# Self-products of 4096 rows on one core: adjacent rows for a partition, the last tile outside the loop, and its last columns in sixteen small stores

## The chip, the cores and the metric

One NeuronCore of a Trainium2 chip. The metric is the device time of the whole program in microseconds, median of several executions. The other cores are idle.

## The reference

```python
# inputs: (4096, 256) float32
dot = jnp.einsum('bi,bj->bij', inputs, inputs)
iu, ju = jnp.triu_indices(256)
return dot[:, iu, ju]                 # (4096, 32896) float32
```

Every row gives its 256 x 257 / 2 = 32896 products. 4.19 MB come in, 538.97 MB go out.

## The kernel before

A batch tile is 128 rows, one row for a partition. A row's products are 256 runs: run i is `x[i:]` times the scalar `x[i]`. VectorE and ScalarE share the runs, and a third of the 32896 columns is collected in each of three output buffers, then stored by one DMA from the sync engine's queue. Tile 0 is written out ahead of the loop, tiles 1 to 31 are the loop.

```python
x_in = x.rearrange("(g p) d -> p g d", p=P)          # tile g = rows 128 g to 128 g + 127
x_out = [v.rearrange("(g p) c -> g p c", p=P) for v in dram_disjoint_views(out, PIECES)]
xt = xpool.tile([P, groups, d], F32, name="x")
cuts = [0, 1, groups // 2, groups]
for a, b in zip(cuts, cuts[1:]):
    nc.sync.dma_start(xt[:, a:b], x_in[:, a:b])      # three input loads
...
def batch_tile(x_of, g, first):
    for c, (lo, hi) in enumerate(zip(borders, borders[1:])):
        o = opool.tile([P, hi - lo], F32, tag=f"o{c}", name=f"o{c}")   # bufs=1
        cuts = [lo, *(first if c == 0 else []), hi]
        for a, b in zip(cuts, cuts[1:]):
            shares.even()
            for _, i, j, at, length in runs(d, a, b):
                shares.multiply(o[:, at - lo : at - lo + length], x_of, j, i, length)
            dest = x_out[c][bass.ds(g, 1), :, a:b].rearrange("o p c -> p (o c)")
            nc.sync.dma_start(dest, o[:, a - lo : b - lo])

batch_tile([xt[:, 0], xt[:, 0]], 0, FIRST)
with tc.For_i(1, groups, 1, ..., iteration_sync="reg_based") as g:
    ...                                              # copies of x for each engine
    batch_tile([xv, xa], g, [])
```

## Time and profile before

| | before |
|---|---|
| time, median | 1292.98 us (1292.86 when the prediction was made) |
| profiled span | 1290.7 us |
| read and written | 4.19 and 538.97 MB, 421 GB/s over the span |
| busy VectorE, ScalarE | 77%, 76% |
| loop period, from landing records | 39.8 us |

The time is read from the stores, not from the compute rows; the prediction shows the lines. The landing records of this kernel hold 1632 additions to semaphores for its 102 DMAs, 16 for each; a DMA's landing is here the moment of the last one. They are read as one from each of the 16 DMA engines: of the run's last store 15 come between 1279.10 and 1279.27 us, and one at 1289.10, when the DMA share has long been that of a single engine (0.05). Two more views of the page of the kernel before are used below. First the DMA issues (size in KB, then us from issue to landing), of which the input loads matter:

```profile
x<-in_r_inputs_dram SPq DMA_DIRECT2D x1, 2048.0 KB, 13.6
...
x<-in_r_inputs_dram SPq DMA_DIRECT2D x1, 1920.0 KB, 8.2
```

Both loads are issued within the first 2 us, so the larger number is about the moment at which all input has landed: 15.3 us. The stores land after it, from 16.97 us on. Second, who made VectorE wait (total us, times, longest us):

```profile
DVE o L52 <- DMA out_dram<-o: 259.7, 62, 4.8
```

62 waits in 31 trips, none over 4.8 us: VectorE waits for the landing that frees a buffer twice a trip. That is 260 of its 300 us of idle time; most of the rest is the end, when its work is done and the stores still run.

### The profile page before, as it was taken

What the parts mean: (1) busy time and instruction counts of PE and PEld (TensorE: products, weight loads), DVE (VectorE), ACT (ScalarE), POOL (GpSimd) and SP (SyncE); (2) the same over time, 40 slices, a digit from 0 to 9 for tenths busy, and PEclk for the clock granted to TensorE, in tenths of its full rate; (3) what the DMA queues carried; (4) which work ended last, traced back from release to release, by engine and by line L of the source; (5) the groups of instructions that cost most, each with busy time, mean ns of one, the idle gap of its engine ahead of it and who ended that gap; (6) DMA issues with size and microseconds to landing.
All of it is one profiled execution on the core that took longest, in us unless ns stands there. A gap on an engine that the chain in (4) does not pass through costs nothing.

```text
span 1290.7 us, 9881 instructions
## 1 busy us (share of the span) xinstructions
DVE 990.8 (77%) x4992; ACT 981.0 (76%) x3330; POOL 0.2 (0%) x4
## 2 busy tenths in 40 slices
DVE  9878787787877788777878778787787877788771
ACT  9778787787877788777878778787787877788771
POOL 0000000000000000000000000000000000000000
DMA  9999999999999999999999999999999999999996
GB/s 373 433 434 432 433 435 434 432 435 434 433 433 435 416 434 416 413 435 434 415 413 435 423 424 415 424 424 433 415 413 435 413 433 415 434 415 413 435 424 259
DMA packets 18405, 543.21 MB, mean 421 GB/s; under 512 B 1632, under 2 KB 5728, under 8 KB 5856
## 3 DMA queue, kind: packets, MB, share of 16 engines
q1 hardware_dynamic: 18400, 543.17, 98.0%
q14 instruction: 5, 0.04, 0.0%
HBM read 4.19 MB, written 538.97 MB: 421 GB/s over the span
## 4 chain that ended last, share of the span: by engine, by line
DMA 59%; DVE 38%; issue 0%; DVEq 0%; SPq 0%
DMA out_dram<-o 59%; DVE o L52 38%; DMA x<-in_r_inputs_dram 0%; DVEq L52 0%; SPq L108 0%; DVEq L112 0%; DVEq L149 0%; DVEq L122 0%
## 5 line engine op out<-in xcount | busy, mean ns | idle before, releaser
L52 DVE TENSOR_SCALAR o<-xv 128x256 f32<-128x256 f32 (+63 forms) x4805 | 951.2, 281 | 267.1 <-DMA out_dram<-o 259.7
L58 ACT ACTIVATE o<-xa 128x255 f32<-128x255 f32 (+63 forms) x3193 | 936.6, 386 | 278.6 <-DMA out_dram<-o 272.4
L52 DVE TENSOR_SCALAR o<-x 128x150 f32<-128x150 f32 (+50 forms) x156 | 30.6, 279 | 3.0 <-DMA x<-in_r_inputs_dram 3.0
L58 ACT ACTIVATE o<-x 128x255 f32<-128x255 f32 (+52 forms) x105 | 30.4, 385 | 0.9 <-DMA x<-in_r_inputs_dram 0.9
L124 ACT ACTIVATE xa<-x 128x256 f32 x31 | 12.9, 416 | 3.4
L122 DVE COPY xv<-x 128x256 f32 x31 | 9.1, 294 | 4.0
L58 ACT ACT_TABLE_LOAD x1 | 1.3, 1283 | 0.7 <-PEq L140 0.7
L140 POOL MEMSET const-bfloat16-1.0<- 128x1 bf16 x1 | 0.1, 101 | 0.0
L140 POOL MEMSET const-uint8-127<- 128x1 uint8 x1 | 0.1, 101 | 0.0
L140 POOL MEMSET const-float32-0.0<- 128x1 f32 x1 | 0.1, 98 | 0.2 <-issue 0.2
L140 POOL MEMSET const-float32-1.0<- 128x1 f32 x1 | 0.1, 98 | 0.0
## 6 DMA issues: line engine op xcount, KB each, us to landing
out_dram<-o SPq DMA_DIRECT2D x63, 5472.0 KB, 30.1
out_dram<-o SPq DMA_DIRECT2D x32, 5504.0 KB, 24.7
x<-in_r_inputs_dram SPq DMA_DIRECT2D x1, 2048.0 KB, 13.6
out_dram<-o SPq DMA_DIRECT2D x1, 2048.0 KB, 14.2
x<-in_r_inputs_dram SPq DMA_DIRECT2D x1, 1920.0 KB, 8.2
out_dram<-o SPq DMA_DIRECT2D x1, 1888.0 KB, 18.2
out_dram<-o SPq DMA_DIRECT2D x1, 1024.0 KB, 9.9
out_dram<-o SPq DMA_DIRECT2D x1, 512.0 KB, 13.1
```

What stands on the lines that cost most here:

```text
L52: self.nc.vector.tensor_scalar(dst, x[:, j : j + length], x[:, i : i + 1], None, ALU.mult)
L58: self.nc.scalar.activation(dst, x[:, j : j + length], AF.Copy, scale=x[:, i : i + 1])
L122: nc.vector.tensor_copy(xv, now)
L124: nc.scalar.activation(xa, now, AF.Copy)
L140: nc = _bacc.Bacc("TRN2", target_bir_lowering=False, num_devices=1)
```

## The change

Its intent, as far as the text tells: make each partition's input contiguous; write the last tile out so that its stores can be shaped; and shape the last ones, perhaps so that the DMA engines end together.

```diff
-    x_in = x.rearrange("(g p) d -> p g d", p=P)
+    x_in = x.rearrange("(p g) d -> p g d", p=P)
...
-        v.rearrange("(g p) c -> g p c", p=P) for v in dram_disjoint_views(out, PIECES)
+        v.rearrange("(p g) c -> g p c", p=P) for v in dram_disjoint_views(out, PIECES)
...
+                if b == width and last:
+                    b -= LAST                                   # LAST = 256
+                store(c, g, a, b, o[:, a - lo : b - lo])
+        if last:
+            p0 = 0
+            for k in [*range(1, 16), 8]:
+                store(c, g, b, hi, o[p0 : p0 + k, b - lo :], p0, p0 + k)
+                p0 += k
...
-        groups,
+        groups - 1,
...
+    final = xt[:, groups - 1]
+    batch_tile([final, final], groups - 1, [], last=True)
```

More of the change, by code (lines that the diff above doesn't have):

```diff
@@ L63 @@
 PIECES = 3
+LAST = 256
 FIRST = [1024, 3072, 7168]
@@ L97, with store, batch_tile @@
     shares = Shares(nc)
-    def batch_tile(x_of, g, first: list[int]):
+    def store(c, g, a, b, src, p0=0, p1=P):
+        dest = x_out[c][bass.ds(g, 1), p0:p1, a:b].rearrange("o p c -> p (o c)")
+        nc.sync.dma_start(dest, src)
+    def batch_tile(x_of, g, first: list[int], last: bool = False):
         for c, (lo, hi) in enumerate(zip(borders, borders[1:])):
@@ L106, in batch_tile @@
                     shares.multiply(o[:, at - lo : at - lo + length], x_of, j, i, length)
-                dest = x_out[c][bass.ds(g, 1), :, a:b].rearrange("o p c -> p (o c)")
-                nc.sync.dma_start(dest, o[:, a - lo : b - lo])
+                if b == width and last:
[6 more added lines that the diff above has]
+                p0 += k
     batch_tile([xt[:, 0], xt[:, 0]], 0, FIRST)
```

## The prediction

> **What bounds the kernel now.** I read the page first (busy rows, DMA rows, queues), then the sync engine's waits, then a table of stretches over the end, then the landing and packet records of single DMAs in the trace.
>
> ```profile
> DVE  9878787787877788777878778787787877788771
> ACT  9778787787877788777878778787787877788771
> DMA  9999999999999999999999999999999999999996
> GB/s 373 433 434 432 433 435 434 432 435 434 433 433 435 416 434 416 413 435 434 415 413 435 423 424 415 424 424 433 415 413 435 413 433 415 434 415 413 435 424 259
> ...
> q1 hardware_dynamic: 18400, 543.17, 98.0%
> ```
>
> The reader is to see that VectorE and ScalarE are idle a quarter of the time, that the 16 DMA engines are busy in every slice but the last, and that the ceiling is about 435 GB/s. 538.97 MB must be written, so the kernel is bound by its stores. Compute only has to stay ahead of them.
>
> ```profile
> SPq L108 <- DVE o L52: 1192.2, 96, 19.2
> SPq L112 <- DMA out_dram<-o: 23.6, 2, 12.9
> SPq L108 <- ACT o L58: 4.2, 2, 3.9
> ```
>
> The second line matters most. At the loop's exit the sync engine waits 23.6 us for the landings of the last trip's DMAs. In this kernel nothing follows the loop, so that wait is only the drain [...].
>
> ```profile
> 1264.90:1276.10 11.20, 0.00 (x0) 0.00 (x0) 0.00 (x0) 1.00 1.02 440
> 1276.10:1279.30 3.20, 0.00 (x0) 0.00 (x0) 0.00 (x0) 1.00 0.54 234
> 1279.30:1289.10 9.80, 0.00 (x0) 0.00 (x0) 0.00 (x0) 1.00 0.05 22
> 1289.10:1290.70 1.60, 0.00 (x0) 0.00 (x0) 0.00 (x0) 1.00 0.00 0
> ```
>
> (Columns: stretch, length, busy of VectorE, ScalarE, GpSimd, clock, DMA share, GB/s.) In the last 9.8 us of transfers the share is 0.05, one engine of 16. The landing records say the same of the whole run: each DMA adds 16 to its semaphore, and the last addition falls behind the median one by 0.4 us for the input, 2.4 us in the first trips, 6.3 us at 240 us, and about 10.5 us from the middle of the run on, where the single set of output buffers stops it growing. A fast engine needs 24 packets of 1.618 us = 38.8 us for a trip; the slow one needs 39.84 us, which is the period of the loop. That slow engine never idles between 3 us and 1289.1 us, so it sets the time. Its packets take about 1.67 us while VectorE and ScalarE run and 1.62 us while they idle.
>
> [...]
>
> **The change part by part.**
>
> *Row mapping.* A partition's 32 rows are adjacent, so the second and third input loads become one piece of 15 KB and one of 16 KB for a partition in place of 31 of 1 KB. In the records, the 248 pieces of an engine took from 2.93 to 14.8 us, 11.85 us for 4.06 MB. At the 434 GB/s that stores reach this is 9.36 us. The stores queue behind the loads without a gap (landings at 16, 18.6, 23.4, 27.9, 40.8, 53.8 us), and their data is ready in time (issues at 10.5, 18.8, 33.6 us, the last one limited by compute, all ahead of their turn even if the queue is 2.5 us earlier). So the slow engine's whole chain moves forward: **-2.5 us**. The SBUF side of the stores is the same. On the HBM side the pitch is 32 x 131584 B = 4112 KiB = 4 MiB + 16 KiB, and I take the rate as unchanged.
>
> *The last tile outside the loop.* The order of the changed program shows that the sync engine's branch out of the loop waits for all three store semaphores of the loop and for a barrier of all engines, and that VectorE's and ScalarE's last tile comes after this barrier. So the 23.6 us wait, harmless before, now stands in the middle: no compute of tile 31 and no store of it until the slow engine has landed tile 30. The stall of the slow engine, from its last packet of tile 30 to its first of tile 31:
> - last packet's end to landing, 0.46 us (1288.64 to 1289.10 at the end of before);
> - barrier, 0.55 us (last landing 1289.12, release 1289.67);
> [...]
> - compute of the first third before anything can be stored, 7.4 us (1225.55 to 1232.93 in the last trip);
> - issue to first packet, 1.0 us (0.74 to 1.76 us at the start).
>
> Sum **+9.9 us**. After that the queue stays full: the second store is issued 8.5 us and the third 23.5 us after the first, while two stores take 25.9 us. The tile itself takes the slow engine what it took before (39.4 us from landing to landing), less 1 KB for each of 8 partitions if that engine gets no small store: **-0.3 us**.
>
> *The 16 small stores.* Seven of them (1 to 7 partitions) go out right behind the main store and hide under it. [...] the order shows the store of 8 partitions waiting for lane 3, which is that of the last 10752-column store. It can be issued only when the slow engine has landed that. The stores of 8 to 15 partitions then follow one another at 0.44 to 0.47 us (the spacing of issues at 9.53, 10.00 and 10.47 us), and the final one of 8 partitions shares lane 3 with the first of 8. Its issue comes 8 x 0.44 = 3.5 us after the main landing; issue to landing about 1.9 us (1.0 to the first packet, 0.4 for its latency as in the first load's packets, 0.5 to the landing). **+5.4 us**, with almost no bytes: 128 KB.
>
> Sum: 1292.86 - 2.5 + 9.9 - 0.3 + 5.4 = 1305.4, so I say **1305 us**, a ratio of 1.009.
>
> **The rivals.**
> 1. *HBM addresses decide.* [...] If that took 5% of the store rate, the time would be about 1305 + 62 = 1367 us. [...] About 7%.
> 2. *The slow engine is cured.* If its slowness came from the addresses of the rows that it writes, the new mapping would give 38.8 us a trip: about 31 x 1.0 us less, 1305 - 31 = 1274 us, still within 2%. Against: its packets are slow exactly while compute runs, and in the last 9.8 us, when nothing else runs, its packets follow at 1.624 us; that is no property of addresses. About 5%.
> 3. *The drain is hidden.* If the lag of the slow engine, or the last tile's compute, could run across the barrier, the stall would vanish and the kernel would gain: 1292.9 - 2.5 - 0.3 + 5.4 = 1295.5 us, or 1290 us if the small stores hid too. Against: the waits in the order. About 5%.
> 4. *The small stores even out the end*, which is perhaps their intent: [...] after the drain the lag starts from zero and is only about 1 us in one tile.
>
> **Range and chances.** The uncertain terms within my account are [...] the tail of small stores (3 to 8 us, since the issue cost of a DMA with 8 to 15 partitions isn't in the trace), and the gain of the loads (1 to 3 us). Together some 4 us to either side; rivals 2 and 3 pull the low end further. Range 1297 to 1311 us. Slower by over 2% means above 1318.7 us, which only rival 1 gives: 0.07. Faster by over 2% means below 1267.0 us, which would need rival 2 and hidden stalls at once: 0.03. Within 2%: 0.90.
>
> **What the profile will show.** The input loads landing at about 12.5 us in place of 15.3. A loop period of 39.8 us as before. VectorE and ScalarE idle for over 10 us before the last tile, with the DMA share falling to one engine and then to 0 for about 8 us near 1250 us; the sync engine's wait at the loop's exit shorter than the span's end. A last tile whose slow engine trails by 1 us, not 10. Then some 5 us at the end with nearly no bytes, stores 8 to 15 spaced by under half a microsecond. A changed period of the loop would prove me wrong about addresses; a busy DMA row straight through 1250 us would prove me wrong about the drain; a last store that lands right after the main one would prove me wrong about the lanes.

What is cut out told of the hardware what no trace or run had shown: which engines a DMA runs on, what a large pitch does, rules for semaphores and drains. One term of the sum is among it, my guess of 0.5 us for the jump to the code behind the loop. The four terms of the stall that are left make 9.4 us (0.46 + 0.55 + 7.4 + 1.0); with the cut one the stall came to +9.9 and the whole to 1305.4 us, as it stands. A lane is the semaphore to which a DMA reports: in the trace of the kernel before, the nine DMAs ahead of the loop report to eight semaphores in turn, the ninth to that of the first; the lanes are counted from 0.

## The result, and the profile after

1304.89 us (1304.81 to 1305.06, 4 runs) against 1292.98 us: a ratio of 1.0092, 95% interval 1.0075 to 1.011. All ratios here are the mean time of one kernel's fast runs over that of the other's of the same rounds, so not quite the ratio of the medians quoted. By the 2% rule this is "same"; by the interval it is clearly a little slower. The result was correct.

The sync engine's waits of the changed kernel (total us, times, longest us):

```profile
SPq L125 <- DMA out_dram<-o: 23.5, 2, 12.9
SPq L103 <- DMA out_dram<-o: 10.7, 1, 10.7
```

The first line is the 23.6 us drain of before, unchanged, but work now follows it. The second is new: one store waited 10.7 us for another to land. It is the store of 8 partitions: in the trace it waits for the semaphore of the main store, to which it reports too; the main store landed at 1297.55 us, and this one was issued at 1297.56. Next, what ended VectorE's waits in the changed kernel:

```profile
DVE o L52 <- DMA out_dram<-o: 250.3, 59, 4.8
DVE o L52 <- PEq L165: 25.2, 1, 25.2
DVE o L52 <- DVE xv L135: 6.8, 29, 0.2
```

The second line is a wait that the kernel before did not have: once, for 25.2 us. It names TensorE, which does no work in this kernel. That is the barrier at the loop's exit, put down to whoever updated its semaphore last; what held the barrier was the sync engine, and what held the sync engine was the landing of tile 30 (1248.33 us; the first product of tile 31 starts at 1249.16). Here is where an inferred releaser has to be followed one step further.

Stretches of the end of the changed kernel (length, busy of VectorE, ScalarE, GpSimd, clock, DMA share, GB/s):

```profile
1238.60:1247.90 9.30, 0.00 (x0) 0.00 (x0) 0.00 (x0) 1.00 0.05 24
1247.90:1257.50 9.60, 8.25 (x34) 8.34 (x23) 0.00 (x0) 1.00 0.00 1
1257.50:1296.10 38.60, 22.25 (x122) 21.65 (x82) 0.00 (x0) 1.00 1.01 433
1296.10:1297.20 1.10, 0.00 (x0) 0.00 (x0) 0.00 (x0) 1.00 0.10 24
1297.20:1301.90 4.70, 0.00 (x0) 0.00 (x0) 0.00 (x0) 1.00 0.09 22
1301.90:1303.10 1.20, 0.00 (x0) 0.00 (x0) 0.00 (x0) 1.00 0.00 0
```

This is the whole story in six lines. The slow engine drains tile 30 alone (share 0.05); nothing moves for 9.6 us while the first third of tile 31 is computed; the last tile is stored at 433 GB/s; the slow engine ends about 1 us after the others, not 10; then 4.7 us at 22 GB/s for the small stores.

### The profile page after: what moved, and what is told of

It reads as the page before. It is cut to its first block, busy times and chain, and to the rows that moved or that the text cites. A ratio compares the mean times of both kernels' runs of the same rounds, so it can differ in the third digit from the quotient of the medians.

```text
span 1303.1 us, 9865 instructions
## 1 busy us (share of the span) xinstructions
DVE 990.3 (76%) x4991; ACT 980.4 (75%) x3329; POOL 0.2 (0%) x4
## 5 line engine op out<-in xcount | busy, mean ns | idle before, releaser
L52 DVE TENSOR_SCALAR o<-xv 128x256 f32<-128x256 f32 (+63 forms) x4650 | 920.5, 282 | 257.5 <-DMA out_dram<-o 250.3
L58 ACT ACTIVATE o<-xa 128x255 f32<-128x255 f32 (+63 forms) x3090 | 906.4, 386 | 268.7 <-DMA out_dram<-o 262.7
L52 DVE TENSOR_SCALAR o<-x 128x249 f32<-128x249 f32 (+34 forms) x311 | 61.1, 281 | 28.1 <-PEq L165 25.2
L58 ACT ACTIVATE o<-x 128x18 f32<-128x18 f32 (+50 forms) x208 | 60.4, 383 | 26.0 <-PEq L165 25.1
L137 ACT ACTIVATE xa<-x 128x256 f32 x30 | 12.5, 416 | 3.3
```

Of the source, the lines that this page charges most:

```text
L52: self.nc.vector.tensor_scalar(dst, x[:, j : j + length], x[:, i : i + 1], None, ALU.mult)
L58: self.nc.scalar.activation(dst, x[:, j : j + length], AF.Copy, scale=x[:, i : i + 1])
L137: nc.scalar.activation(xa, now, AF.Copy)
```

## The experiments

Twelve kernels were run. "Mapping alone" is the kernel before with only the two `rearrange` lines changed.

### Taking the change apart

**Mapping alone.**

```diff
-x.rearrange("(g p) d -> p g d", p=P)
+x.rearrange("(p g) d -> p g d", p=P)        # and the same for the output
```

> The mapping alone, in the kernel before (loop over all 31 further tiles, no last tile outside, no small stores). Theory (the mapping only shortens the input loads, and the store period stays 39.8 us): in the changed kernel the loop's landing of tile 30 came 1.40 us earlier than before (1248.33 against 1249.73), so 1292.98 - 1.4 = 1291.6 us, ratio 0.9989. Rival A (the 4112 KiB pitch also changes the store rate, hidden in the sum): a loop period off 39.8 us by more than 0.1 us and a time off by more than 3 us. Rival B (the mapping is neutral): 1293.0 us.

Measured: 1291.82 us against 1292.98, ratio 0.999 (0.9977 to 1.0004). The interval includes 1, but every one of the five runs (1291.6 to 1291.93) lies below every one of before (1292.92 to 1293.29). The loads' lines are now

```profile
x<-in_r_inputs_dram SPq DMA_DIRECT2D x1, 2048.0 KB, 12.6
...
x<-in_r_inputs_dram SPq DMA_DIRECT2D x1, 1920.0 KB, 7.0
```

1.0 and 1.2 us shorter. Two stretches of the loop of 39.84 us each, 400 us apart, are both filled by the work of one trip:

```profile
500.00:539.84 39.84, 30.94 (x157) 30.59 (x105) 0.00 (x0) 1.00 0.98 423
900.00:939.84 39.84, 30.97 (x157) 30.61 (x105) 0.00 (x0) 1.00 0.98 423
```

The first of them in the kernel before:

```profile
500.00:539.84 39.84, 30.95 (x158) 30.60 (x106) 0.00 (x0) 1.00 0.99 424
```

The landing records measure the period itself: it is (1288.16 - 54.16) / 31 = 39.81 us; the kernel before has (1289.10 - 55.42) / 31 = 39.80. So the HBM addresses of the stores changed nothing, and the gain is the loads'.

**The last tile outside the loop alone** (old mapping, whole stores).

```diff
-        groups,
+        groups - 1,
...
+    final = xt[:, groups - 1]
+    batch_tile([final, final], groups - 1, [])
```

> The last tile outside the loop alone: old mapping, whole stores. Theory (drain and barrier put the last tile's first third of compute between two stores): from the landing of tile 30 to that of tile 31 the changed kernel took 49.22 us, the kernel before 39.37, so +9.85 us, less nothing for small stores: 1292.98 + 9.9 = 1302.9 us, ratio 1.0077. Rival (the cost of the change sits in the small stores, the last tile is hidden by the stores still queued): 1293 to 1294 us.

Measured: 1301.91 us, ratio 1.007 (1.0056 to 1.0084): +8.9 us, a microsecond less than expected. The landings of tiles 30 and 31 are 49.51 us apart (1249.55 and 1299.06), close to the 49.22 foreseen, but the span ends 1.1 us after the last landing, not 1.6 as before: the loop-exit barrier that used to stand after the last landing is now in the stall. I had counted it as new. That is about half of the microsecond; the rest is not explained.

**Mapping and last tile, without the small stores.**

```diff
-    batch_tile([final, final], groups - 1, [], last=True)
+    batch_tile([final, final], groups - 1, [])
```

> The changed kernel without its small stores (the last store whole, 11008 columns). Theory: 1292.98 - 1.4 + 9.9 = 1301.5 us, which is 3.4 us below the changed kernel. Rival (the small stores are free because they are 128 KB in 543 MB): 1304.9 us.

Measured: 1300.7 us, ratio 1.0059. The parts add up: 1291.82 + 8.93 = 1300.75. The small stores therefore cost 1304.89 - 1300.7 = 4.2 us.

**Four small stores in place of sixteen.**

```diff
-            for k in [*range(1, 16), 8]:
+            for k in [32] * 4:
```

> The changed kernel with the last 256 columns in four stores of 32 partitions in place of 16 stores of 1 to 15 and 8. Same bytes, but lanes 4 to 7 are free, so no small store waits for the main one. Theory (the tail is the wait for lane 3 and the issues after it): all four land right behind the main store, 1301.5 us plus at most 0.5, that is 1301.5 to 1302.0. Rival (each small store costs by itself, 4.3 us for 16): a quarter of the tail stays, 1302.4 to 1302.8 us. Rival (rows of 1 KB are what costs): 1304.9 us.

Measured: 1300.96 us, 0.3 us above the kernel with no small stores. The same 128 KB in the same rows of 1 KB cost almost nothing once no store has to wait for a lane. Its end:

```profile
1296.40:1297.70 1.30, 0.00 (x0) 0.00 (x0) 0.00 (x0) 1.00 0.19 57
1297.70:1299.00 1.30, 0.00 (x0) 0.00 (x0) 0.00 (x0) 1.00 0.00 0
```

The last bytes have moved by 1297.4 us, the last store has landed at 1298.14, and the program ends at 1299.0; the 4.7 us of trickle are gone. So bytes and row length cost 0.3 us at most, and "a quarter of the tail for a quarter of the stores" is wrong too. The run changes the number of stores and their shape together with the lanes. That the lane is the cause is read from the changed kernel itself: after its wait of 10.7 us nine stores are issued one behind the other, in 3.3 us, and in this run no store waits so.

### What the stall is made of

**Two tiles outside the loop** (small stores as in the change).

```diff
-        groups - 1,
+        groups - 2,
...
+    final = xt[:, groups - 2]
+    batch_tile([final, final], groups - 2, [])
     final = xt[:, groups - 1]
```

> The changed kernel with two tiles outside the loop in place of one (small stores as in the change). Theory (the cost is one drain and barrier at the loop's exit, whatever follows it): no second stall, 1304.9 us give or take 0.5. Rival (code outside the loop is slow by itself[...]): a second stall of up to 8.9 us, 1310 to 1314 us.

Measured: 1304.33 us, half a microsecond *below* the changed kernel. One drain, one stall:

```profile
1198.60:1208.50 9.90, 0.00 (x0) 0.00 (x0) 0.00 (x0) 1.00 0.05 22
1208.50:1217.90 9.40, 8.43 (x35) 8.53 (x23) 0.00 (x0) 1.00 0.18 75
1217.90:1297.30 79.40, 52.56 (x276) 51.47 (x184) 0.00 (x0) 1.00 0.96 414
```

The picture is that of the changed kernel, one tile earlier, and the two tiles after it run through at 414 GB/s. Code outside the loop is not slow here; leaving the loop is what costs, 9.4 us in this run.

**The first third of the last tile in four stores.**

```diff
-    batch_tile([final, final], groups - 1, [], last=True)
+    batch_tile([final, final], groups - 1, FIRST, last=True)     # [1024, 3072, 7168]
```

> The changed kernel with the first third of the last tile cut into stores of 1024, 2048, 4096 and 3776 columns as in the first tile, so that the first store of the last tile waits for 0.9 us of compute and not for 7.5. Theory (compute of the first third is the largest part of the stall): the stores now start 6.5 us earlier, but the last third's data is ready only 29 us after the barrier, as before (the main store was issued at 1278.06 and its engines were still busy until 1283.9); the main store then begins 1 us after its issue and lands at about 1292.8 in place of 1297.55: 1304.9 - 4.8 = 1300.1 us. Rival (the stall is the barrier and the jump, not compute): 1304 to 1305 us.

Measured: 1299.27 us, 5.6 us below the changed kernel where 4.8 was expected; the main store landed at 1292.39 us (expected 1292.8). The stall:

```profile
1247.90:1250.90 3.00, 1.57 (x6) 1.66 (x5) 0.00 (x0) 1.00 0.01 3
```

By 1250.9 us five or six products of each engine are made, and the first packet follows at 1251.1, not 1257.5. So most of the stall was the 7.5 us of compute behind the barrier, and the old lesson of tile 0 (cut the first store small) holds after this drain too, for 5.6 us. It doesn't give back the whole stall because the last third's data is then what is late: all 16 engines end the main store within 0.14 us of one another, none of them lagging.

### Where the slow DMA engine comes from

**Almost no compute in the loop** (mapping alone). Its output is wrong, which doesn't matter for the time.

```diff
-                for _, i, j, at, length in runs(d, a, b):
+                for _, i, j, at, length in list(runs(d, a, b))[:most]:   # 2 in the loop
```

(The three output buffers are allocated once, so that what is stored has been written.)

> The mapping alone with only the first two of each third's products computed in the loop; a wrong result on purpose, same stores, same waits, almost no VectorE and ScalarE work. Theory (the slow engine's packets are stretched from 1.62 to 1.67 us by running compute): the lag hardly grows, the period is 38.8 to 38.9 us, time 1260 to 1263 us. Rival (that engine is slow by itself or by its rows' addresses): 1291.8 us, lag of 10 us at the end.

Measured: 1263.82 us, ratio 0.9774. A trip:

```profile
500.00:538.90 38.90, 1.17 (x4) 1.81 (x4) 0.00 (x0) 1.00 1.00 433
```

The stores are the same bytes to the same addresses, now at 433 GB/s in place of 423, and the last engine trails the median one by 0.6 us at the end, not by 10. The period from landings is (1260.36 - 54.43) / 31 = 38.90 us. Running compute is what makes one engine slow here: 39.81 us a trip with it, 38.90 without. The run also lets the store queue get deeper, but the earlier packets of the kernel before (1.67 us beside compute, 1.62 us without, on a queue that never emptied) say that depth isn't it.

**One engine's compute only** (same). Their outputs are wrong, which doesn't matter for the times.

```diff
+            if only == "scalar":      # in the vector branch; "vector" in the scalar branch
+                return                # all but the first two products of a third
```

> The mapping alone with ScalarE's products left out of the loop but the first one of each third; a wrong result on purpose. Without compute in the loop the slow engine kept pace (38.9 us a trip), with both engines' compute it lost 1.0 us a trip. Theory (any compute traffic stretches it, in proportion): with VectorE alone a loss of about 0.5 us a trip, period 39.3 us, time about 1277 us. Rival (ScalarE's traffic alone does it): 1263 us. Rival (VectorE's alone): 1291.8 us.

> The counterpart: VectorE's products left out of the loop but the first one of each third; wrong on purpose. Theory (in proportion): about 1277 us. Rival (ScalarE's traffic alone does it): 1291.8 us. Rival (VectorE's alone): 1263 us.

Measured: 1280.41 us with VectorE alone and 1274.69 us with ScalarE alone. By their landings the periods are (1277.01 - 54.45) / 31 = 39.44 and (1271.22 - 54.63) / 31 = 39.24 us, which is 0.54 and 0.34 us over the run without compute; with both, 39.81, it is 0.91. The two add up to 0.88, near the 0.91 of both; the split is less even than the half each that was expected. What in the compute does it (its traffic in the buffers or its count of instructions) is not told apart; the cause inside the chip is open. Loading of instructions is not it: the profile of the kernel before has five packets of that in the whole run. It is not tested whether the recording of instructions takes part: every run comes with a span, so none is known to be without it.

**Stores of 64 partitions** (mapping alone).

```diff
+                for q in (0, 64):
+                    dest = x_out[c][bass.ds(g, 1), q : q + 64, a:b].rearrange("o p c -> p (o c)")
+                    nc.sync.dma_start(dest, o[q : q + 64, a - lo : b - lo])
```

> The mapping alone with each store as two of 64 partitions. [...] Theory E (one of the DMA engines is slow whatever it reads): lag and loop period as before, 39.8 us, time 1291.8 us. Theory P (the partitions that the slow engine reads are slow): [...] the lag grows by 0.5 us a trip and not by 1.0, the period is about 39.3 us, time 1276 us.

(How the partitions of the halves fall to the DMA engines was assumed in theory P, not shown.)

Measured: 1839.01 and 1856.21 us in two runs; two more, 1882.24 and 1894.2, are over 1.5% above the fastest. All are a miss of both theories. The run of 1856.21 us:

```profile
DMA  9999999999999999999999999999999999999997
...
DMA packets 16277, 543.22 MB, mean 293 GB/s; under 512 B 3216, under 2 KB 3344, under 8 KB 3472
```

The engines look just as busy, but move 293 GB/s in place of 421. I had not foreseen it, and why stores of half the partitions are so slow isn't shown: the page counts as many packets of 512 B and more as that of the mapping alone (13061 in both). Whether the slow engine or its partitions are at fault stays open: this run can't tell.

### An attempt to use it

Four small packets follow the slow engine's last main packet in the changed kernel (1297.12 to 1297.26 us). The stores of 1 to 7 partitions had been queued by then, so this engine got a row of four of the seven. I tried to spare it work by giving some to three others. That a store of 123 partitions runs on three engines, and that the slow one isn't among them, was an assumption; no run had shown it by then.

```diff
+                if b == width and not first:
+                    parts = [(0, P, a, b - TAIL), (0, 123, b - TAIL, b), (123, P, b - TAIL, b)]   # TAIL = 128
```

> The mapping alone, and in each trip the last 128 columns of the third store go out in a store of 123 partitions [...] and one of 5. [...] period 39.7 us, time 1287 to 1290 us. [...] If small stores cost more in the loop than their packets, over 1292 us.

(The time is for a slow engine outside the three.)

Measured: 1369.54 us, ratio 1.0593. None of the forecasts: a wait took over. The sync engine's longest:

```profile
SPq L113 <- DMA out_dram<-o: 862.1, 31, 28.0
```

28 us in each of 31 trips. The order of instructions shows the store of 123 partitions waiting for the main store before it: with the tile number in a register, two stores to one view of the output are not known to be disjoint. The second try gives the tails views of their own:

```diff
-dram_disjoint_views(out, PIECES)
+dram_disjoint_views(out, PIECES + 2)        # views 3 and 4 for the tail stores
```

> The same as the run before, but the tail stores go to views of the output that the program knows to be disjoint from the main store's, so they no longer wait for the main store to land (that wait, 28 us a trip, decided the run before). Theory [...]: the period lies between 39.65 and 39.85 us[...]; time 1287 to 1292 us, at best a gain of a few us on the mapping alone. [...]

(My estimate for the three was 39.8 us a trip: the 38.8 us of a fast engine's packets in the kernel before, and about 1 us assumed for a batch.)

Measured: 1299.68 us, ratio 1.0052. The wait is gone:

```profile
SPq L113 <- DVE o L52: 1147.1, 130, 17.8
SPq L117 <- DMA out_dram<-o: 24.3, 2, 23.4
```

but no gain: the time is nearly 8 us above the top of what was expected. At the end, three engines each ran 42 packets of 512 B (41 of the one store, one of the other), about 1.0 us a batch, and two more engines ran one packet each. The slowest, 12 us behind, is one of the three. Its period rose to about 40 us, (1293.88 - 54.4) / 31, where I had put the three at 39.8: the 24 large packets of a fast engine took 39.0 us in the kernel before (1026.7 to 1065.7 us), not 38.8, and a batch adds 1.0. The old slow engine can be followed from packet to packet in this trace, from 1000.4 to 1081.5 us: it never idles, its large packets take 1.61 to 1.73 us, and it runs one packet of 512 B a trip (a trip is 39.73 us). So the batches show that the store of 123 partitions ran on three engines (41 rows each), that these are among the five of the other store, and that the original slow engine isn't one of the three; sparing it only moved the bound. Its number is not shown, since the trace names no engines. No version with a correct result beat the mapping alone, 1291.82 us.

## Why the prediction was right, step by step

Predicted 1305.4 (said: 1305), measured 1304.89. The sum was better than its terms, so its closeness is in part luck. In the profiled executions the difference is 1303.1 - 1290.7 = 12.4 us, and it splits so:

| term | predicted | measured | from |
|---|---|---|---|
| mapping | -2.5 | -1.4 | landing of tile 30: 1248.33 against 1249.73 |
| stall | +9.9 | +9.6 | slow engine's packets: end 1247.87, next start 1257.51 |
| last tile on the slow engine | -0.3 | +0.2 | 39.60 us of packets against 39.37 |
| tail of small stores | +5.4 | +4.4 | landings 1297.55 and 1301.90 |
| after the last landing | 0 | -0.4 | 1.20 us against 1.62 |
| sum | +12.5 | +12.4 | |

- *What bounds it:* right. The slow engine's period is untouched by the change (39.80 us) and by the mapping (39.81, before 39.80), and the run without compute (38.90) confirms that its lag comes from compute. The fast engines were put too low: the 24 packets of a trip took 39.0 us in the kernel before, not 24 x 1.618 = 38.8.
- *Mapping:* the mechanism was right, the size was off by half. I took the loads at the stores' 434 GB/s. Measured, the two loads ran at 1.966 MB in 5.47 us and 2.097 MB in 5.72 us (landings 2.89, 8.36, 14.08), that is 359 and 367 GB/s: most packets of the loads take 0.57 or 0.61 us, but some take up to 1.28 us, at the start of the first of the two and in the second half of the second. The alone run puts the gain at 1.2 us.
- *Stall:* right in its parts: landing 0.46, barrier 0.52, jump 0.3 (the term of 0.5 was a guess), compute 7.47, first packet 0.84 us. But the barrier was no new cost; it moved, and the end became shorter by it. The kernel with only the last tile outside shows the net: 8.9 us.
- *The last tile:* I expected the slow engine to get none of the small stores, hence less work. It got four of the first seven, and it was slightly slower, probably because compute runs beside more of this tile's stores: some 22 us of them here, 15 in the last trip of before.
- *Tail:* right in mechanism, by the wait of 10.7 us and the four-store run; 1.0 us too large. The stores of 8 to 15 partitions followed each other at 0.32 to 0.42 us (their issue took 0.28 us for 8 partitions, rising to 0.38 for 15; the issues of 2 to 7 partitions behind the running main store took 1.0 to 1.2 us), and the last one landed 1.32 us after its issue, not 1.9.
- *Rivals:* addresses (rival 1) fell with the mapping alone; the cure (rival 2) fell with the unchanged period; the hidden drain (rival 3) fell with the last tile alone; the evening-out (rival 4) works in the wrong direction here, since the slow engine gets its share (four packets of the first seven stores).

The errors of the mapping (1.1 us) and of the tail (1.0 us) have opposite signs in the sum. With the range from 1297 to 1311 us neither would have mattered alone.

## What to carry to other kernels

Code moved out of the loop was not a continuation of it here: at a loop's exit look for what the issuing engine waits for (23.5 us), because the drain that the kernel before had at its end cost a full pipeline fill when it stood in the middle (9 us, most of it the compute ahead of the first store, of which a smaller first store gives back 5.6). Count DMAs against their lanes: with sixteen small stores on eight lanes the one of 8 partitions waited 10.7 us for the big one, and the sixteen cost 4.2 us for 128 KB that four stores move for 0.3. And when a bandwidth-bound kernel falls short of its best slices (421 against 435 GB/s here), read the landing of each DMA engine by itself; here one slow engine of sixteen set the pace, at 39.8 us a trip where a fast one needed 39.0.
